# A new table of places for a two-layer kernel whose engines run from orders written out in advance

## The chip, the cores and the metric

The kernel runs on one core of one Trainium2 chip. The metric is the device time of one execution in microseconds (us), from the first to the last instruction with what little lies around it. The data are float32 throughout.

## What is computed

The input x has 128 images of 128 channels and 32 x 32 pixels (1024 pixels to an image). Two layers follow each other.

Layer 0 is attention over the 128 images at each pixel, with four heads, an output projection, a residual and a layer norm. Its result is written to DRAM as `mid`.

Layer 1 works on each image by itself. It multiplies by a 128 x 128 matrix (`cv1`); one branch is a 3 x 3 depthwise convolution with a batch norm and SiLU (`l`); the other is a layer norm over channels followed by a Mamba block over the 1024 pixels. Cut to what matters here, the Mamba block is:

```
xm, z = split(t @ in_proj.T)              # 256 channels each
xm    = silu(conv1d(xm))                  # causal, 4 taps
dt, B, C = split(xm @ x_proj.T)           # 8, 16, 16 columns
dt    = softplus(dt @ dt_proj.T + bias)   # 256 channels
h     = exp(dt * A) * h + dt * B * xm     # over pixels, for 256 channels x 16 states
y     = sum over states of h * C, + xm * D
out   = (y * silu(z)) @ out_proj.T
```

The two branches meet in a last matrix (`cv2`), and x is added.

## The kernel before

Layer 0 (`attention_layer`) is not touched by the change. Layer 1 (`mamba_layer`) goes image by image. The state recurrence of one image has 256 x 16 = 4096 rows of 1024 pixels, cut into 32 **groups** of 128 rows. Group k belongs to a half h of the channels (k < 16: h = 0, else h = 1), to a block nb of four states (k // 4 mod 4) and to a block db of 32 channels (k mod 4). For each group:

- ScalarE makes the decays exp(dt * A) from `dtr`, which holds dt replicated over the states (`decays`, L1058).
- The inputs dt * B * xm come from GpSimd for two groups at once (`inputs(j)` for groups 2j and 2j+1, into `dbu`, L1069), from `dtxr` (dt * xm replicated) and `brep` (B replicated). For nb = 0, that is groups 0 to 3 and 16 to 19, TensorE makes them instead (`inputs_by_tensor`, L1080) from the transposed `dtxT` and the diagonal matrices `bdiag`; then the decays of the group are written into `dbu`.
- VectorE runs the recurrence as a scan (`group`, L1093).
- The product with C (`crep`) is GpSimd's for the groups in `ON_POOL` (`product`, L1100), else VectorE's, right behind the scan (L1095).
- TensorE adds up the products of four groups at a time (`sums`, L1116), and at the end of each half VectorE multiplies by the gate (`gate`, L1125).

`dbu` has two buffers: inputs j overwrite what inputs j-2 (or the decays of groups 2j-4 and 2j-3) left, so inputs j wait for scan 2j-3. `hc`, in which products stand, has eight. PSUM leaves two banks (`banks`, "p_ps" in the profile) for everything else.

The replicated tiles are loaded by DMA from DRAM: dt and dt * xm of one half are stored (`dt_store`, `dtx_store`), and then loaded four times over in sets of four DMAs of 256 KB each: `dtr[0]`, `dtr[1]` (`load_dt`), `dtxr[0]`, `dtxr[1]` (`load_dtx`). B and C are stored with `bc_store` and loaded by `load_b` (brep) and `load_c` (crep). All DMAs are issued by SyncE, in one queue. `x_load` brings the image after the next, `x_again` brings back the present one for its last addition.

All else for the next images goes on beside the recurrence: the outputs of the image before (`o_mm`, `o_copy`, `out_store`), the second part of the next image (`d_mm`, `b_mm`, `a_mm`, `split`, `expm`, `log1p`, `dt_mm`, `dt_copy`, `dtx_mul`, the transposes `t_mm`, `t_copy`, the depthwise `taps`, `z_mm`, `diagonals`), and the first part of the one after it (`cv1_mm`, `squared`, `variance`, `rstd`, `normed`, `xm_mm`, `xm_copy`, `padded`). `dtx_mul` is GpSimd's, `normed` VectorE's, copies and functions are ScalarE's.

No scheduler decides the order; `step` writes it out by hand, once per image, with a loop over k. Each engine runs its instructions in exactly that order. In step k come, one after the other: the operations whose place is below k + 0.3; the scan of group k; the gate; the decays of group k + 2 (with TensorE's inputs); after an odd k GpSimd's inputs for groups k + 3 and k + 4; the operations whose place is below k + 0.6; the product of group k; the loads for which `LOADS_*` names k; the sums for which `SUMS_AT` names k. `PLACES` gives the place of each operation, by its name and its count within the image; an operation whose predecessors aren't in yet, or for which no PSUM bank is free, comes as soon as it may (`Order.put`). The entries of `LOADS_DT` and `LOADS_DTX` are, in order: h = 1 parts 0 and 1 of the present image, h = 0 parts 0 and 1 of the next.

The core of the loop, shortened:

```
for k in range(NG):
    order.put(k + EARLY)
    group(k)
    ...
    if k % 2 and (2 * a < NG or nxt is not None):
        if not by_tensor(2 * a):
            inputs(a % (NG // 2))
    order.put(k + LATE + EARLY)
    product(k)
    for ahead, do, what, at in LOADS:
        if k == at and (nxt is not None or not ahead):
            do(nxt if ahead else im, *what)
```

Of the kernel before, what the change touches and what calls it, by code (L numbers as in the profile page):

```python
# [320 lines left out]
class Bank:  # L321
# [7 lines left out]
EARLY, LATE, LAST = 0.3, 0.3, 0.6  # L329


ON_POOL = [2, 3, 8, 10, 12, 13, 14, 15, 16, 17, 22, 24, 25, 28, 29, 30, 31]
SHARED = 5
SUMS_AT = [6, 9, 11, 19, 20, 23, 29]
GATES_AT = [20, 1]
LOADS_DT = [12, 13, 27, 30]
LOADS_DTX = [15, 18, 31, 31]
LOADS_B = [23, 3, 4]
LOADS_C = [25, 0]
REMADE = 18  # L340

PLACES = {
    "silus": [3.3],
    "o_mm": [5, 10.3],
    "o_copy": [5.01, 10.31],
    "out_store": [5.02, 10.34],
    "d_mm": [5.03],
    "d_copy": [7],
    "t_mm": [7.01, 8, 20.02, 28],
    "t_copy": [7.02, 8.02, 20.03, 28.02],  # L350
    "a_mm": [8.3, 8.01, 28.01, 30],
    "split": [8.31, 8.03, 28.03, 30.01],
    "expm": [8.32, 30.02],
    "b_mm": [9.3],
    "b_copy": [9.31],
    "z_mm": [10.32, 10.35, 16.01, 14],
    "z_copy": [10.33, 11.3, 16.02, 14.01],
    "log1p": [12, 30.03],
    "dt_mm": [12.01, 12.02, 31.61, 31.63],
    "dt_copy": [13.3, 15.3, 31.62, 31.64],  # L360
    "dt_store": [15.31, 31.66],
    "x_load": [16],
    "dtx_mul": [16.3, 31.65],
    "dtx_store": [16.31, 31.67],
    "bc_store": [18],
    "diagonals": [
        26.3, 24.3, 20.32, 18.06, 18.04, 18.07, 22.04, 18.01, 29.3, 18.02, 18.03, 19, 25.3, 24,
        21, 18.05,
    ],
    "taps": [19.01, 19.3, 19.31],  # L370
    "l_copy": [19.32, 19.33],
    "cv1_mm": [20, 22.01, 25.01, 27],
    "squared": [20.01, 22.02],
    "variance": [20.3, 22.31],
    "rstd": [20.31, 23.3],
    "normed": [22, 25],
    "xm_mm": [22.03, 30.04, 25.03, 25.04],
    "xm_copy": [22.3, 31.6, 26, 26.31],
    "padded": [25.02, 27.02],
    "x_again": [27.01],  # L380
}


# [203 lines left out]
def mamba_layer(ctx: ExitStack, tc: tile.TileContext, ident, eps, mid, c, out):  # L587
# [398 lines left out]
    def load_x(b):  # L986
        nc.sync.dma_start(x, mid[ds(b, 1)].rearrange("o c l -> (o c) l"))
# [39 lines left out]
    def on_pool(k):  # L1027
        return k in ON_POOL

# [138 lines left out]

    LOADS = [(i > 1, load_dt, (1 - i // 2, i % 2), v) for i, v in enumerate(LOADS_DT)]
    LOADS += [(i > 1, load_dtx, (1 - i // 2, i % 2), v) for i, v in enumerate(LOADS_DTX)]  # L1170
    LOADS += [(i == 0, load_b, (i,), v) for i, v in enumerate(LOADS_B)]
    LOADS += [(i < 1, load_c, (i,), v) for i, v in enumerate(LOADS_C)]
    SUMS = {v: j for j, v in enumerate(SUMS_AT)}

    def step(b, im, nxt=None, was=None, then=None):
# [23 lines left out]
        if then is not None:  # L1199
            ops.append(Op("x_load", lambda: load_x(then), stored_outputs))  # L1200
            ops += first_part(im, [*reads, ops[-1]], xm_start=SUMS_AT[4] + LAST)

        users = [op for op in ops if op.name == "cv1_mm"] or stored_outputs
        ops.append(Op("x_again", lambda: load_x(b), users))
        order = Order(ops, banks, PLACES)
        for k in range(NG):
# [170 lines left out]
```

## Time and profile before

| | |
|---|---|
| median of 3 runs | 16214.31 us (16213.59 to 16221.85) |
| the profiled execution: time, span | 16207.52 us, 16205.7 us |
| TensorE (PE) busy | 14907.9 us, 92% |
| VectorE (DVE) busy | 14001.0 us, 86% |
| ScalarE (ACT) busy | 11943.2 us, 74% |
| GpSimd (POOL) busy | 13178.7 us, 81%; from slice 8 of 40 on, 90% or more in each |
| DMA | 2187.55 MB, mean 135 GB/s |
| granted TensorE clock | 0.960 |

The profile is of one execution. Layer 0 takes the first seven or so of its 40 slices, and layer 1 the rest, where GpSimd shows 9 tenths in every slice. PE, DVE, ACT, POOL and SP are TensorE, VectorE, ScalarE, GpSimd and SyncE; L1069 is line 1069 of the kernel. In the lines of groups, the numbers after the bar are busy time and the mean of one in ns, then the engine's idle time just before them and what ended it. In the lines of waits: total us, how many times, longest. In a timeline: start, duration, engine, line, operation, tiles, how many in a row, and in brackets the idle time before it and its releaser. "SPq" is SyncE's queue of DMAs, at their issue.

### The profile page before, as it was taken

How to read it: one execution, taken by the hardware profiler on the slowest of the kernel's cores; microseconds unless marked ns; L12 is line 12 of the kernel's file. 1: busy time of each engine (PE TensorE's matmuls, PEld its weight loads, DVE VectorE, ACT ScalarE, POOL GpSimd, SP SyncE). 2: the span in 40 equal slices, each digit the busy share in tenths (PEclk: the TensorE clock that was granted, in tenths of full speed). 3: DMA queues.
4: the chain of work that ended last, by engine and by line, in shares of the span. 5: the costliest groups of instructions: out<-in, count | busy, mean ns of one | idle time of the engine just before them, and what ended most of it. 6: DMA issues, size and time to landing. Idle time of an engine off the chain costs nothing. (4 is left out here: it accounts for less than half of the span.)

```text
span 16205.7 us, 335746 instructions
## 1 busy us (share of the span) xinstructions
PE 14907.9 (92%) x141366; PEld 7196.6 (44%) x141366; DVE 14001.0 (86%) x8882; ACT 11943.2 (74%) x17542; POOL 13178.7 (81%) x4488
## 2 busy tenths in 40 slices
PE   9999999899999999999999999999999999999998
PEld 6666666343444434444444444444444444443443
DVE  7777777698888889999989999989999899889988
ACT  6666666677777777777777777777777777777776
POOL 1222222699999999999999999999999999999999
PEclk9999999899999999999999999999999999999998
DMA  3222221566666666666666666666666666666665
GB/s 57 53 43 53 53 43 33 130 152 153 155 158 155 152 153 156 155 157 157 156 157 157 154 152 154 156 158 157 154 152 154 152 158 155 157 151 152 155 158 131
DMA packets 1175599, 2187.55 MB, mean 135 GB/s; under 512 B 656848, under 2 KB 657888, under 8 KB 1174112
## 3 DMA queue, kind: packets, MB, share of 16 engines
q1 hardware_dynamic: 1174112, 2166.24, 54.5%
q8 instruction: 1114, 18.25, 0.5%
q14 instruction: 373, 3.06, 0.1%
HBM read 1746.30 MB, written 419.43 MB: 134 GB/s over the span
## 5 line engine op out<-in xcount | busy, mean ns | idle before, releaser
L1069 POOL TENSOR_TENSOR dbu<-dtxr,brep 128x2048 f32<-128x2048 f32 x1536 | 6971.2, 4544 | 453.4 <-DMA dtxr<-dtxd 265.7
L1100 POOL TENSOR_TENSOR hc<-hc,crep 128x1024 f32<-128x1024 f32 x2176 | 5122.3, 2374 | 0.0
L1058 ACT ACTIVATE da<-dtr,aneg 128x1024 f32<-128x1024 f32 x2944 | 3283.3, 1117 | 1246.6 <-DVE hc L1093 719.3
L1093 DVE TENSOR_TENSOR_SCAN hc<-da,dbu 128x1024 f32<-128x1024 f32 x1664 | 3753.9, 2278 | 360.5 <-POOL dbu L1069 300.3
L1093 DVE TENSOR_TENSOR_SCAN da<-da,dbu 128x1024 f32<-128x1024 f32 x1280 | 2922.1, 2283 | 357.5 <-POOL dbu L1069 352.6
L1095 DVE TENSOR_TENSOR hc<-da,crep 128x1024 f32<-128x1024 f32 x1792 | 2194.4, 1225 | 161.9 <-PE y_ps L1116 58.9
L1116 PE MATMUL y_ps<-hc,fold 128*32 128x512 f32 x16384 | 2244.8, 646 | 43.3 <-POOL hc L1100 39.2
L1080 PE MATMUL da<-bdiag,dtxT 128*32 128x128 f32 x65536 | 1987.4, 275 | 196.9 <-issue 93.9
L1080 PEld LDWEIGHTS da<-bdiag,dtxT 128*32 128x32 f32 x65536 | 1776.9, 110 | 574.4 <-DVE hc L1093 374.7
L730 PE MATMUL p_ps<-tn,wk 128*128 128x512 f32 x4056 | 1821.2, 596 | 0.0
L1093 DVE TENSOR_TENSOR_SCAN da<-dbu,da 128x1024 f32<-128x1024 f32 x512 | 1172.5, 2290 | 212.4 <-PE da L1080 123.6
L964 ACT ACTIVATE bdiag<-ident,bT 128x128 f32<-128x128 f32 x4096 | 1307.8, 387 | 65.0 <-PE da L1080 64.2
L1093 DVE TENSOR_TENSOR_SCAN hc<-dbu,da 128x1024 f32<-128x1024 f32 x512 | 1145.1, 2275 | 159.4 <-PE da L1080 113.2
L221 POOL COPY xg<-xt 128x512 f32<-128x512 f32 x256 | 269.8, 1055 | 1236.8 <-PE m_ps L217 1205.7
L730 PEld LDWEIGHTS p_ps<-tn,wk 128*128 128x128 f32 x4056 | 752.8, 189 | 1016.6 <-issue 842.3
L1058 ACT ACTIVATE dbu<-dtr,aneg 128x1024 f32<-128x1024 f32 x1024 | 1119.4, 1142 | 112.5 <-DMA dtr<-dtd 105.6
L1116 PEld LDWEIGHTS y_ps<-hc,fold 128*32 128x32 f32 x16384 | 489.3, 115 | 1542.5 <-issue 1186.3
L243 POOL TENSOR_SCALAR yt<-z,nw,nb 128x512 f32<-128x512 f32 x256 | 319.8, 1249 | 1029.6 <-DVE z L242 1029.6
L915 PE MATMUL p_ps<-xpad,dwd 64*64 64x512 f32 x9216 | 1046.0, 592 | 25.6 <-issue 24.8
L790 POOL TENSOR_TENSOR sp<-dt,xm 128x1024 f32<-128x1024 f32 x256 | 613.0, 2395 | 270.8 <-ACT dt L804 264.6
L767 PE MATMUL p_ps<-xp,dtwT 8*128 8x512 f32 x1016 | 643.8, 716 | 204.4 <-ACT dtxT L832 174.4
L203 DVE TENSOR_TENSOR oT<-m_ps,rden 128x512 f32<-128x512 f32 x256 | 177.1, 692 | 575.7 <-ACT rden L202 575.7
(200 smaller groups left out, 22410.7 us busy)
## 6 DMA issues: line engine op xcount, KB each, us to landing
dtr<-dtd SPq DMA_DIRECT2D x2048, 256.0 KB, 5.0
dtxr<-dtxd SPq DMA_DIRECT2D x2048, 256.0 KB, 7.3
crep<-bcd SPq DMA_DIRECT2D x1024, 256.0 KB, 6.7
brep<-bcd SPq DMA_DIRECT2D x1536, 128.0 KB, 5.0
x<-mid SPq DMA_DIRECT2D x256, 512.0 KB, 5.7
dtd<-dt SPq DMA_DIRECT2D x256, 512.0 KB, 4.8
dtxd<-sp SPq DMA_DIRECT2D x256, 512.0 KB, 6.9
xt<-in_x SPq DMA_DIRECT2D x64, 1024.0 KB, 12.0
```

Source lines behind the costliest of these rows:

```text
L730: nc.tensor.matmul(bank.tile, lhsT=wk[:, k, h * P : (h + 1) * P], rhs=tn[:, c * CH + k : (c + 1) * CH + k], start=k == 0, stop=c > 0 and k ...
L767: nc.tensor.matmul(bank.tile, lhsT=dtwT[c * HP + XD : c * HP + NX, h * P : (h + 1) * P], rhs=xp[c * HP + XD : c * HP + NX], start=True, st ...
L790: nc.gpsimd.tensor_mul(sp, dt, im["xm"][h])
L915: nc.tensor.matmul(pair[r] .tile[c * HP : (c + 1) * HP] .rearrange("p (r q) -> p r q", q=HH), lhsT=dwd[rs, k, :], rhs=xpad[rs, y0 : y0 + r ...
L964: nc.scalar.activation(bdiag[:, j, :], ident, AF.Copy, scale=bT[:, j : j + 1])
L1058: nc.scalar.activation(operands(k)[0], dtr[db // 2][:, db % 2, :], AF.Exp, scale=aneg[:, h * NDB + db, nb : nb + 1])
L1069: nc.gpsimd.tensor_mul(dbu[j % 2], dtxr[db // 2], b.unsqueeze(1).to_broadcast([P, 2, L]))
L1080: nc.tensor.matmul(operands(k)[1][n * GD : (n + 1) * GD, tb * P : (tb + 1) * P], lhsT=dtxT[:, tb, db * GD : (db + 1) * GD], rhs=bdiag[:, t ...
L1093: nc.vector.tensor_tensor_scan(dst, a, b, 0.0, ALU.mult, ALU.add)
L1095: nc.vector.tensor_mul(hc[k % 8], dst, crep[nb // 2][:, nb % 2, :])
L1100: nc.gpsimd.tensor_mul(hc[k % 8], hc[k % 8], crep[nb // 2][:, nb % 2, :])
L1116: nc.tensor.matmul(y_ps[db * GD : (db + 1) * GD, chunk(c)], lhsT=fold, rhs=hc[(j * NDB + db) % 8][:, chunk(c)], start=False, stop=nb == NN ...
```

## The change

Only constants change: the groups whose products are GpSimd's, the steps of the sums, the steps of the loads, and the table of places. No instruction is added or taken away; the order on each engine changes. Compared by the built programs, in one image in the middle:

- GpSimd multiplies groups 7, 9 and 26 instead of 8, 10 and 25. Its order by kinds of instruction stays the same but for one: the first dtx_mul comes before product 14 instead of before product 16.
- SyncE's order before: crep[1]; brep[1]; brep[2]; out_store; out_store; dtr[0], dtr[1] (h = 1); dt_store; dtxr[0]; x_load; dtx_store; bc_store; dtxr[1]; brep[0]; crep[0]; x_again; dtr[0], dtr[1]; dtxr[0], dtxr[1] (h = 0 of the next image); dt_store; dtx_store.
- SyncE's order after: brep[2]; brep[1]; crep[1]; bc_store; out_store; out_store; x_load; dtr[0], dtr[1] (h = 1); dt_store; dtxr[0]; dtxr[1]; brep[0]; dtx_store; crep[0]; dtxr[0] (h = 0 of the next image); x_again; dtr[0]; dtr[1]; dtxr[1]; dtx_store; dt_store.
- On TensorE the second o_mm moves from behind sums 1 to behind sums 0, and dt_mm, z_mm, t_mm and a_mm are dealt anew among steps 7 to 16; from step 17 on its order by kinds is the same.
- On ScalarE both first dt_copy come before decay 16 (one stood before decay 16, one behind decay 17), expm and log1p before decay 13 (log1p stood behind it), o_copy of the second chunk before decay 11 (it stood behind decay 12), and the diagonals are spread over steps 18 to 25 instead of 18 to 29.

```diff
-ON_POOL = [2, 3, 8, 10, 12, 13, 14, 15, 16, 17, 22, 24, 25, 28, 29, 30, 31]
+ON_POOL = [2, 3, 7, 9, 12, 13, 14, 15, 16, 17, 22, 24, 26, 28, 29, 30, 31]
 SHARED = 5
-SUMS_AT = [6, 9, 11, 19, 20, 23, 29]
+SUMS_AT = [6, 11, 13, 19, 21, 23, 28]
 GATES_AT = [20, 1]
-LOADS_DT = [12, 13, 27, 30]
-LOADS_DTX = [15, 18, 31, 31]
-LOADS_B = [23, 3, 4]
-LOADS_C = [25, 0]
+LOADS_DT = [13, 13, 27, 29]
+LOADS_DTX = [14, 18, 26, 31]
+LOADS_B = [23, 3, 1]
+LOADS_C = [25, 3]
 REMADE = 18
 
 PLACES = {
+    "o_mm": [2, 8.3],
     "silus": [3.3],
-    "o_mm": [5, 10.3],
-    "o_copy": [5.01, 10.31],
-    "out_store": [5.02, 10.34],
-    "d_mm": [5.03],
-    "d_copy": [7],
-    "t_mm": [7.01, 8, 20.02, 28],
-    "t_copy": [7.02, 8.02, 20.03, 28.02],
-    "a_mm": [8.3, 8.01, 28.01, 30],
-    "split": [8.31, 8.03, 28.03, 30.01],
-    "expm": [8.32, 30.02],
-    "b_mm": [9.3],
-    "b_copy": [9.31],
-    "z_mm": [10.32, 10.35, 16.01, 14],
-    "z_copy": [10.33, 11.3, 16.02, 14.01],
-    "log1p": [12, 30.03],
-    "dt_mm": [12.01, 12.02, 31.61, 31.63],
-    "dt_copy": [13.3, 15.3, 31.62, 31.64],
-    "dt_store": [15.31, 31.66],
-    "x_load": [16],
-    "dtx_mul": [16.3, 31.65],
-    "dtx_store": [16.31, 31.67],
-    "bc_store": [18],
+    "d_mm": [3.31],
+    "d_copy": [5.3],
+    "bc_store": [5.31],
+    "o_copy": [6.3, 8.31],
+    "out_store": [6.31, 8.34],
+    "t_mm": [7, 10, 27.3, 20.03],
+    "t_copy": [7.01, 10.01, 27.32, 20.04],
+    "z_mm": [12, 16, 8.32, 12.3],
+    "z_copy": [12.01, 16.01, 8.33, 12.31],
+    "x_load": [8.35],
+    "b_mm": [9],
+    "b_copy": [9.01],
+    "a_mm": [11, 10.02, 27.31, 30],
+    "split": [11.01, 10.03, 27.33, 30.01],
+    "expm": [11.02, 30.02],
+    "log1p": [11.03, 30.03],
+    "dt_mm": [14.02, 14, 31.62, 31.6],
+    "dt_copy": [14.03, 14.01, 31.63, 31.61],
+    "dtx_mul": [14.04, 31.64],
+    "dt_store": [14.05, 31.66],
     "diagonals": [
...
     ],
-    "taps": [19.01, 19.3, 19.31],
-    "l_copy": [19.32, 19.33],
-    "cv1_mm": [20, 22.01, 25.01, 27],
-    "squared": [20.01, 22.02],
-    "variance": [20.3, 22.31],
-    "rstd": [20.31, 23.3],
-    "normed": [22, 25],
-    "xm_mm": [22.03, 30.04, 25.03, 25.04],
-    "xm_copy": [22.3, 31.6, 26, 26.31],
-    "padded": [25.02, 27.02],
-    "x_again": [27.01],
+    "taps": [19.3, 19.31, 19.32],
+    "l_copy": [19.33, 20],
+    "cv1_mm": [20.01, 22.01, 27.02, 25.04],
+    "squared": [20.02, 22.02],
+    "variance": [20.3, 23.3],
+    "rstd": [20.31, 23.31],
+    "normed": [22, 25.03],
+    "xm_mm": [30.04, 22.03, 27, 26],
+    "xm_copy": [30.05, 23, 27.01, 26.01],
+    "dtx_store": [24, 31.65],
+    "padded": [27.04, 25.05],
+    "x_again": [27.03],
 }
```

More of the change, by code (lines that the diff above doesn't have):

```diff
@@ L366 @@
+    "x_load": [8.35],
[9 more added lines that the diff above has]
+    "dt_store": [14.05, 31.66],
     "diagonals": [
-        26.3, 24.3, 20.32, 18.06, 18.04, 18.07, 22.04, 18.01, 29.3, 18.02, 18.03, 19, 25.3, 24,
-        21, 18.05,
-    ],
@@ L370 @@
-    "taps": [19.01, 19.3, 19.31],
-    "l_copy": [19.32, 19.33],
-    "cv1_mm": [20, 22.01, 25.01, 27],
-    "squared": [20.01, 22.02],
-    "variance": [20.3, 22.31],
-    "rstd": [20.31, 23.3],
-    "normed": [22, 25],
-    "xm_mm": [22.03, 30.04, 25.03, 25.04],
-    "xm_copy": [22.3, 31.6, 26, 26.31],
-    "padded": [25.02, 27.02],
-    "x_again": [27.01],
+        25.01, 18.06, 18.07, 18.01, 18.03, 18, 18.04, 25, 18.02, 21.3, 21.31, 25.02, 20.32, 21,
+        21.01, 18.05,
+    ],
+    "taps": [19.3, 19.31, 19.32],
```

## The prediction

> **What bounds the kernel now.** I read the page's costliest groups first, then the waits, then the timelines of one image. In the groups, GpSimd's two kinds of product stand at the top:
>
> ```profile
> L1069 POOL TENSOR_TENSOR dbu<-dtxr,brep 128x2048 f32<-128x2048 f32 x1536 | 6971.2, 4544 | 453.4 <-DMA dtxr<-dtxd 265.7
> L1100 POOL TENSOR_TENSOR hc<-hc,crep 128x1024 f32<-128x1024 f32 x2176 | 5122.3, 2374 | 0.0
> ```
>
> Per image that is 12 x 4.54 + 17 x 2.37 + two dtx_mul of 2.40 = 99.7 us; they overlap a little in the pipeline and occupy 98.7 us. From one image to the next it is 103.2 us (the 256 gates of L1125 start between 3038.9 and 16194.8 us, two per image: 13155.9 / 127.5). So GpSimd, idle some 4.5 us per image, is the bound, and its idle time is all that a new order can give back. The list of waits says who ends it:
>
> ```profile
> POOL dbu L1069 <- DMA dtxr<-dtxd: 265.7, 256, 3.2
> POOL sp L790 <- ACT dt L804: 264.6, 125, 58.7
> POOL dbu L1069 <- DVE da L1093: 127.4, 100, 20.8
> ```
>
> The first is 2.08 us per image. I call t0 the end of inputs 15 and t1 the end of inputs 7, the last input products of the two halves of an image. GpSimd's timeline of one image shows where the waits lie:
>
> ```profile
> 9093.33 4.54 POOL L1069 TENSOR_TENSOR dbu<-dtxr,brep 128x2048 f32<-128x2048 f32 x1
> ...
> 9113.89 4.55 POOL L1069 TENSOR_TENSOR dbu<-dtxr,brep 128x2048 f32<-128x2048 f32 x1 [2.05 <-DMA dtxr<-dtxd]
> ...
> 9121.53 9.04 POOL L1069 TENSOR_TENSOR dbu<-dtxr,brep 128x2048 f32<-128x2048 f32 x2 [0.76 <-DMA dtxr<-dtxd]
> ...
> 9146.46 4.53 POOL L1069 TENSOR_TENSOR dbu<-dtxr,brep 128x2048 f32<-128x2048 f32 x1
> ...
> 9161.83 2.41 POOL L790 TENSOR_TENSOR sp<-dt,xm 128x1024 f32<-128x1024 f32 x1 [1.53 <-ACT dt L804]
> 9164.72 4.54 POOL L1069 TENSOR_TENSOR dbu<-dtxr,brep 128x2048 f32<-128x2048 f32 x1 [0.48 <-DMA dtxr<-dtxd]
> ```
>
> Here t1 = 9097.87 and t0 = 9150.99. Inputs 10 and 11 wait 2.05 and 0.76 us for dtxr (over 122 images 1.33 and 0.65), dtx_mul 1 waits 1.53 (always), inputs 2 waits 0.48. Over those images t1 to t0 takes 52.7 us and t0 to the next t1 50.5. Next, SyncE's queue:
>
> ```profile
> 9094.64 5.22 SPq L991 DMA_DIRECT2D dtr<-dtd  x8
> 9104.39 0.34 SPq L979 DMA_DIRECT2D dtd<-dt  x1
> 9104.83 2.71 SPq L991 DMA_DIRECT2D dtxr<-dtxd  x4
> 9107.58 0.42 SPq L987 DMA_DIRECT2D x<-mid  x1
> 9109.53 0.34 SPq L979 DMA_DIRECT2D dtxd<-sp  x1
> ...
> 9111.26 2.73 SPq L991 DMA_DIRECT2D dtxr<-dtxd  x4
> ...
> 9144.59 0.35 SPq L987 DMA_DIRECT2D x<-mid  x1
> 9146.63 6.09 SPq L991 DMA_DIRECT2D dtr<-dtd  x8
> 9152.82 6.71 SPq L991 DMA_DIRECT2D dtxr<-dtxd  x8
> ```
>
> and the windows of 2 us with their last two columns, DMA share and GB/s:
>
> ```profile
> 9141.00:9143.00 2.00, 2.00 (x6) 0.91 (x5) 2.00 (x2) 1.05 (x1) 2.00 (x1) 1.00 0.00 0
> ...
> 9149.00:9151.00 2.00, 2.00 (x6) 0.83 (x5) 0.83 (x1) 1.43 (x3) 2.00 (x2) 1.00 1.03 219
> ```
>
> The transfers come in two bursts, t1-3 to t1+22 and t0-6 to t0+28, in which the DMA engines are full at about 220 GB/s, and are idle between. One set of four loads is 1 MiB, 4.8 us in a full queue. So a load's arrival is set by the bytes issued ahead of it.
>
> **What the Trainium skill says.** [...] "DMA: Bandwidth & Descriptors", section on queues, rings and completion order, says that each DMA engine consumes descriptors in ring order; the trace agrees: after t0 the means of the last landings are x -3.0, dtr[0] 2.4, dtr[1] 7.2, dtxr[0] 12.7, dtxr[1] 17.1, in order of issue. The same page, on the anatomy of one DMA, says that semaphore waits happen on the issuing sequencer: a DMA that waits holds all behind it in SyncE's queue. In the trace, dtxr[0] (9104.83) stands behind the dtd store (9104.39), which waits for ScalarE's dt_copy.
>
> **The change, part by part.** No instruction is added or removed; durations stay.
>
> *Groups.* Products 8, 10, 25 become 7, 9, 26. GpSimd's sequence of kinds stays: one product between inputs 5 and 6, one between 6 and 7, one between 14 and 15. VectorE's multiply moves by one group. Slack: product 25 starts at 9144.15; scan 26 will end at 9136.12 (scan 25's start) + 3.46 (scan with multiply) + 2.2 = 9141.8. Sums 1 now needs product 7, which ends where product 8 does (9086.5), while scan 12, which needs sums 1, starts at 9091.4. Zero, hidden by 2 to 3 us.
>
> *dtx_mul 0* moves ahead of products 14 and 15. It needs dt_copy by t1+4.7; the new places (14, before ScalarE's decay 16) give t1+1.7. Zero.
>
> *Second half.* With dt_copy at t1+1.7, the dtd store and dtxr[0] are issued at once instead of at t1+6.5. But the queue still holds both dtr sets: the last of dtr was issued at 9099.44 and took 6.6 us to land. dtr[0]'s issue follows decay 13, at t1-3.8 in the mean now. In the new order ScalarE has decay 12, split, expm and log1p ahead of it in place of o_copy: group 10's multiply ends 9.15 us after scan 7's end, which is t1-18.2; then 1.05 + 1.2 + 0.94 + 0.95 and decay 13's 1.1 make 14.4, so t1-3.8 again. So dtxr[0] gains only the thin spot in the DMA between (0.3 to 0.5 us). dtxr[1] gains more: x_load, the dtxd store and bc_store, 1.1 MiB, leave the place before it, so that it lands 4.8 us after dtxr[0] instead of 7.7, and inputs 11's 0.65 us goes. Inputs 12 gains 0.1 to 0.2 more, until it meets scan 21. Sum about 1.1 us. What is late next: VectorE's second normed, which already waits for ScalarE,
>
> ```profile
> 9135.45 0.75 DVE L708 SCALAR_TENSOR_TENSOR tn<-p_ps,b1c,tn 128x512 f32<-128x512 f32 x1 [0.26 <-ACT tn L702]
> ```
>
> at the end of TensorE's chain taps, sums 3, cv1, variance. That doesn't move; scan 25 follows it, and inputs 14 must wait for scan 25. Now inputs 14 starts 1.05 us after scan 25's end (mean). So the half gains at most 1.05, and **0.9** allowing for scatter.
>
> *First half.* dtxr[0] of the next image moves from step 31 to 26: behind inputs 14, at t0-6.8, into an idle DMA. It can't be late for inputs 2 any more (0.5 us gone). But it and x now stand ahead of dtr[0], which decay 0 needs. Estimate: data flows from t0-5.9 (0.9 after issue, as for the burst at t1), dtxr[0] 4.8, x 1.5 to 2.3, dtr[0] 4.8, landing 0.9 after its data: t0+6.1 to 6.9, against 2.4 now. Scan 0 waits for that decay already:
>
> ```profile
> 9155.85 2.30 DVE L1093 TENSOR_TENSOR_SCAN da<-dbu,da 128x1024 f32<-128x1024 f32 x1 [0.36 <-ACT dbu L1058]
> ```
>
> It moves from t0+4.9 to t0+7.4 (decay 1.1). From scan 0 to scan 7's end: two scans with multiply at 3.47, gate 1.15, two scans at 2.2, three with multiply at 3.46, one scan 2.3: 25.2 us, so t0+32.6. Inputs 5 reuses scan 7's half of dbu; it starts at t0+31.9 here, 32.3 in the mean, with 0.8 us of slack that is now used up. It starts at 32.65, and 18.15 us later is t1: 50.8 instead of 50.5, a loss of **0.35**; at the late end of my estimate 1.1.
>
> *Behind dtx_mul 1*: its 1.53 us hang on scan 31, inputs of group 33, dt_mm, dt_copy, in the same order: stays. brep[2] and brep[1] go ahead of crep[1]; 0.5 MiB instead of 1 stands before brep[1], and it lands earlier; crep[1] at about t0+28.3, first used by VectorE at t0+33.8. bc_store, x_load, dtx_store 0 go to idle stretches. Diagonals come earlier on ScalarE; squared 1 may be 1 us later, its reader has 3. Zero each.
>
> **Sum.** 0.9 - 0.4 = 0.5 us per image, 127 times: 60 us off the profiled execution's 16207.5. The median of the runs, 16214.3, is 6.8 higher, so about **16155**.
>
> **Rivals.** (1) *dtr[0] decides the other way.* If it lands at t0+7.4, scan 7 ends at 33.9, the half costs 1.65 more, and the gain of the other is 0.6 at the low end: 1.05 x 127 = 133 us slower, 16347. The point where it turns is a landing at t0+6.6, half a us from my estimate; for it speaks that nothing hides scan 0, against it that x drains faster than the loads (256 GB/s at a DMA share of 0.76). (2) *Even*: what inputs 11 saves comes back at inputs 5; 16214. That is also what comes of it if dtxr lands no sooner, since dtr is ahead of it before and after. (3) *A larger gain*: dtr[0] by t0+5.3 costs nothing, the 0.5 at inputs 2 stays won: 1.3 x 127 = 165 us, 16050. All of GpSimd's DMA waits, 2.5 x 127 = 318 us, can't be had because of normed.
>
> **Numbers.** A measurement can tell about 0.2%, 32 us, from no change. My case and (3) together 0.48, even 0.18, slower 0.34. Range 16030 to 16325: from somewhat beyond (3) nearly to (1). The faster cases alone: 16035 to 16180.
>
> **What would show it.** Inputs 11 without a DMA wait; inputs 10 still with one of 0.5 to 1 us; inputs 2 without; dtr[0] landing at t0+6 to 7 and VectorE idle 2.5 to 3 us before scan 0 for ScalarE; inputs 5 waiting for VectorE. Wrong if GpSimd waits for brep or crep, if ScalarE's decays 20 to 27 stop VectorE, or if t1 to t0 stays at 52.7.

## The result, and the profile after

The changed kernel takes **16575.5 us** (median, 16569.9 to 16589.1) against 16218.1 us before on the same chip: 1.0222 times as long, 95% interval 1.0209 to 1.0234. The forecast was 60 us faster; it is 357 us slower. The profiled execution took 16589.1 us, its span is 16587.3 us against 16205.7. The granted TensorE clock was 0.963 in it, against 0.960 before, so the clock is not the cause.

I use the forecast's two marks again: t0 is the end of GpSimd's inputs 15, t1 that of inputs 7. Over the 122 images in the middle of the run, means in us:

| | t0 to t1 | t1 to t0 | one image |
|---|---|---|---|
| before | 50.49 | 52.72 | 103.22 |
| after | 51.64 | 54.59 | 106.23 |

So 3.01 us per image are lost: 1.15 in the first half (t0 to t1) and 1.87 in the second (t1 to t0). Times 127 that is 382 us, the difference of the spans. The costliest groups of the changed kernel (busy time, mean ns of one, then the idle time before them and what ended most of it):

```profile
L1069 POOL TENSOR_TENSOR dbu<-dtxr,brep 128x2048 f32<-128x2048 f32 x1536 | 6982.5, 4546 | 818.7 <-DVE da L1093 429.0
L1100 POOL TENSOR_TENSOR hc<-hc,crep 128x1024 f32<-128x1024 f32 x2176 | 5121.1, 2373 | 0.0
```

GpSimd does the same work in the same time, 4546 and 2373 ns an instruction. What has grown is its idle time before the inputs, 818.7 us instead of 453.4, and most of it now ends with VectorE's scan, not with a DMA. The waits of the changed kernel (total, times, longest; lines left out are marked by dots) say the same:

```profile
...
PEld p_ps L915 <- issue: 760.1, 2214, 5.2
...
ACT dbu L1058 <- DMA dtr<-dtd: 522.7, 278, 5.3
...
DVE da L1093 <- ACT dbu L1058: 443.0, 127, 6.4
...
POOL dbu L1069 <- DVE da L1093: 429.0, 167, 20.8
...
DVE hc L1095 <- PE y_ps L1116: 342.0, 126, 8.5
...
PE da L1080 <- issue: 233.0, 142, 3.0
...
POOL dbu L1069 <- DMA dtxr<-dtxd: 225.9, 205, 2.2
...
POOL dbu L1069 <- DVE hc L1093: 152.8, 130, 1.3
```

The same waits in the kernel before, as far as the forecast does not show them:

```profile
...
PE da L1080 <- issue: 93.9, 60, 3.8
...
DVE da L1093 <- ACT dbu L1058: 88.1, 126, 1.9
...
DVE hc L1095 <- PE y_ps L1116: 58.9, 33, 4.4
...
POOL dbu L1069 <- DVE hc L1093: 3.7, 3, 1.5
```

GpSimd's DMA wait fell from 265.7 to 225.9 us, its wait for VectorE's scans rose from 127.4 to 429.0, and the 152.8 is as good as new (3.7 before). Behind VectorE stand ScalarE (443.0; 88.1 before) and TensorE (342.0; 58.9 before). And TensorE stops by itself: "issue" means that the profile shows nothing it waited for, 233.0 us in 142 stops at L1080 (93.9 in 60 before).

One image of the changed kernel, t0 = 9241.81, t1 = 9292.79, the next t0 = 9346.34. VectorE's and GpSimd's timelines (start, duration, in brackets the idle time before it and what ended it):

```profile
9249.37 2.29 DVE L1093 TENSOR_TENSOR_SCAN da<-dbu,da 128x1024 f32<-128x1024 f32 x1 [3.06 <-ACT dbu L1058]
...
9316.67 1.22 DVE L1095 TENSOR_TENSOR hc<-da,crep 128x1024 f32<-128x1024 f32 x1 [1.51 <-PE y_ps L1116]
...
9331.49 0.75 DVE L708 SCALAR_TENSOR_TENSOR tn<-p_ps,b1c,tn 128x512 f32<-128x512 f32 x1 [0.51 <-ACT tn L702]
```

```profile
9274.65 4.52 POOL L1069 TENSOR_TENSOR dbu<-dtxr,brep 128x2048 f32<-128x2048 f32 x1 [1.20 <-DVE hc L1093]
...
9308.27 4.55 POOL L1069 TENSOR_TENSOR dbu<-dtxr,brep 128x2048 f32<-128x2048 f32 x1 [1.53 <-DMA dtxr<-dtxd]
...
9315.08 4.55 POOL L1069 TENSOR_TENSOR dbu<-dtxr,brep 128x2048 f32<-128x2048 f32 x1
...
9321.37 4.55 POOL L1069 TENSOR_TENSOR dbu<-dtxr,brep 128x2048 f32<-128x2048 f32 x1 [1.74 <-DVE da L1093]
```

The first half's loss is the first line of each: scan 0 waits 3.06 us for its decay, and inputs 5 then wait 1.20 for scan 7. In the second half inputs 10 still wait for DMA (1.53), inputs 11 (9315.08) don't wait any more, as forecast, and inputs 12 (9321.37) wait 1.74 us for scan 21, which they did not in the image shown of before. Scan 21 is late because VectorE's multiply of group 20 waited for TensorE (9316.67). So look at TensorE:

```profile
9300.29 2.38 PE L1080 MATMUL da<-bdiag,dtxT 128*32 128x128 f32 x78
9305.22 1.69 PE L1080 MATMUL da<-bdiag,dtxT 128*32 128x128 f32 x50 [2.54 <-issue]
9306.84 7.96 PE L915 MATMUL p_ps<-xpad,dwd 64*64 64x512 f32 x72
9314.73 1.92 PE L1116 MATMUL y_ps<-hc,fold 128*32 128x512 f32 x16
```

In the inputs of groups 18 and 19, after 78 of their 128 matmuls, TensorE stands still for 2.54 us with nothing to wait for. The taps (L915) and sums 3 (L1116) follow, and the multiply of group 20 writes a buffer of `hc` that sums 3 must have read. I call the sum of such stops per image in the inputs of groups 18 and 19 ("inputs 18, 19" in the expectations below) and the taps **TensorE's gaps**. Counted are the steps of over 0.6 us from the start of one matmul to the start of the next: 0.65 us before, 3.64 after. The taps start at t1+13.5 instead of 11.8 and end at t1+23.0 instead of 20.2.

What does TensorE wait for? The DMA view of the window 9302.3 to 9302.6, with packets, MB and share:

```profile
## 3 DMA queue, kind: packets, MB, share of 16 engines
q1 hardware_dynamic: 17, 0.06, 103.8%
q8 instruction: 1, 0.02, 28.9%
```

Among the data (q1) a DMA of kind "instruction" starts there. In the whole run there are 1114, with 18.25 MB, 16 KB each. They fit TensorE: it executes 141,366 matmuls and as many weight loads, and the Trainium skill ("Trainium Architecture — The Big Picture", The software stack) gives 64 bytes for an instruction, from which I estimate 282,732 x 64 bytes = 18.1 MB. (The same section speaks of the streams as brought in when the program is loaded; here this one comes in blocks of 256 instructions during the run.) This fetch runs from 9302.48 to 9303.86 in the trace, and TensorE goes on at 9305.22, 1.36 us after its end. That is no accident: of the stops in these operations that are longer than 1 us, all 153 in the changed kernel and all 40 in the kernel before end 1.15 to 1.75 us after such a fetch ended, with only two or three such fetches in the 20 us from t1 on. And when all of TensorE's instructions in the trace are numbered from the first, the one with which it goes on is in all 193 stops the third or fourth of a block of 256: each stop stands at the edge of a block as large as one fetch. TensorE had run out of instructions.

SyncE's queue suggests why the fetches are late. The data for t1 to t1+20 are in it sooner:

```profile
9289.13 5.40 SPq L991 DMA_DIRECT2D dtr<-dtd  x8
9294.96 0.34 SPq L979 DMA_DIRECT2D dtd<-dt  x1
9295.39 6.80 SPq L991 DMA_DIRECT2D dtxr<-dtxd  x8
```

Both sets of dtxr are issued right behind dtr, from t1+3.0 to t1+9.8 in the mean; before, they came from t1+6.5 to t1+15.7. The profile counts the fetches among the packets of the same 16 DMA engines. This is **theory A**: the data now stand in the queue while TensorE runs through its shortest instructions (the inputs of groups 16 to 19: 256 matmuls and as many weight loads in 8 us of work, two blocks), and the fetches come late. **Theory B**: the new orders of the engines make the second half longer by themselves. The experiments had to tell these apart, and settle the first half.

### The profile page after: what moved, and what is told of

It reads as the page before. It is cut to its first block, busy times and chain, and to the rows that moved or that the text cites. A ratio compares the mean times of both kernels' runs of the same rounds, so it can differ in the third digit from the quotient of the medians.

```text
span 16587.3 us, 335744 instructions
## 1 busy us (share of the span) xinstructions
PE 14866.6 (90%) x141366; PEld 7183.3 (43%) x141366; DVE 13979.7 (84%) x8882; ACT 11928.1 (72%) x17542; POOL 13180.3 (79%) x4488
## 3 DMA queue, kind: packets, MB, share of 16 engines
q8 instruction: 1114, 18.25, 0.5%
q14 instruction: 374, 3.06, 0.1%
## 5 line engine op out<-in xcount | busy, mean ns | idle before, releaser
L1069 POOL TENSOR_TENSOR dbu<-dtxr,brep 128x2048 f32<-128x2048 f32 x1536 | 6982.5, 4546 | 818.7 <-DVE da L1093 429.0
L1100 POOL TENSOR_TENSOR hc<-hc,crep 128x1024 f32<-128x1024 f32 x2176 | 5121.1, 2373 | 0.0
L1058 ACT ACTIVATE da<-dtr,aneg 128x1024 f32<-128x1024 f32 x2944 | 3283.6, 1116 | 1293.9 <-DVE hc L1093 753.6
L1095 DVE TENSOR_TENSOR hc<-da,crep 128x1024 f32<-128x1024 f32 x1792 | 2194.5, 1225 | 443.8 <-PE y_ps L1116 342.0
L1080 PE MATMUL da<-bdiag,dtxT 128*32 128x128 f32 x65536 | 2037.7, 276 | 522.6 <-issue 233.0
L1116 PE MATMUL y_ps<-hc,fold 128*32 128x512 f32 x16384 | 2174.1, 639 | 37.9 <-POOL hc L1100 35.3
L1080 PEld LDWEIGHTS da<-bdiag,dtxT 128*32 128x32 f32 x65536 | 1791.5, 111 | 929.5 <-DVE hc L1093 362.3
L1093 DVE TENSOR_TENSOR_SCAN da<-dbu,da 128x1024 f32<-128x1024 f32 x512 | 1173.2, 2291 | 702.3 <-ACT dbu L1058 443.0
L1058 ACT ACTIVATE dbu<-dtr,aneg 128x1024 f32<-128x1024 f32 x1024 | 1120.9, 1142 | 665.5 <-DMA dtr<-dtd 522.7
L964 ACT ACTIVATE bdiag<-ident,bT 128x128 f32<-128x128 f32 x4096 | 1251.4, 387 | 190.0 <-PE da L1080 188.9
L915 PE MATMUL p_ps<-xpad,dwd 64*64 64x512 f32 x9216 | 1113.5, 612 | 104.3 <-issue 103.2
L1093 DVE TENSOR_TENSOR_SCAN hc<-dbu,da 128x1024 f32<-128x1024 f32 x512 | 1142.6, 2272 | 42.3 <-PE da L1080 22.4
L1116 PEld LDWEIGHTS y_ps<-hc,fold 128*32 128x32 f32 x16384 | 450.0, 113 | 1570.3 <-issue 1265.5
L870 PE MATMUL p_ps<-xm,xpT 128*64 128x512 f32 x1016 | 392.5, 901 | 435.1 <-ACT xm L842 435.1
L915 PEld LDWEIGHTS p_ps<-xpad,dwd 64*64 64x64 f32 x9216 | 370.4, 137 | 762.0 <-issue 760.1
```

Of the source, the lines that this page charges most:

```text
L870: nc.tensor.matmul(bank.tile[c * HP : (c + 1) * HP], lhsT=xpT[:, h, :], rhs=im["xm"][h][:, chunk(c)], start=h == 0, stop=h == DI2 - 1,)
L915: nc.tensor.matmul(pair[r] .tile[c * HP : (c + 1) * HP] .rearrange("p (r q) -> p r q", q=HH), lhsT=dwd[rs, k, :], rhs=xpad[rs, y0 : y0 + r ...
L964: nc.scalar.activation(bdiag[:, j, :], ident, AF.Copy, scale=bT[:, j : j + 1])
L1058: nc.scalar.activation(operands(k)[0], dtr[db // 2][:, db % 2, :], AF.Exp, scale=aneg[:, h * NDB + db, nb : nb + 1])
L1069: nc.gpsimd.tensor_mul(dbu[j % 2], dtxr[db // 2], b.unsqueeze(1).to_broadcast([P, 2, L]))
L1080: nc.tensor.matmul(operands(k)[1][n * GD : (n + 1) * GD, tb * P : (tb + 1) * P], lhsT=dtxT[:, tb, db * GD : (db + 1) * GD], rhs=bdiag[:, t ...
```

## The experiments

All times and ratios are against the kernel before on the same chip; the means are over the same 122 images. "Gaps" are TensorE's, and the last two columns are counted from t1.

| kernel | time, us | ratio, 95% interval | t0 to t1 | t1 to t0 | gaps | taps end | inputs 12 |
|---|---|---|---|---|---|---|---|
| before | 16218 | 1 | 50.49 | 52.72 | 0.65 | 20.2 | 27.7 |
| after | 16576 | 1.0222 (1.0209 to 1.0234) | 51.64 | 54.59 | 3.64 | 23.0 | 29.6 |
| after, dtxr[0] back | 16486 | 1.0162 (1.0145 to 1.0179) | 50.74 | 54.63 | 3.19 | 23.0 | 29.6 |
| after, dtxd store back | 16510 | 1.0179 (1.0162 to 1.0196) | 51.58 | 53.98 | 2.96 | 22.4 | 29.0 |
| after, four DMAs back | 16415 | 1.0115 (1.0098 to 1.0132) | 50.76 | 54.10 | 2.55 | 22.5 | 29.1 |
| after, dt back too | 16328 | 1.0070 (1.0053 to 1.0086) | 50.56 | 53.61 | 0.79 | 21.6 | 28.6 |
| after, paced | 16572 | 1.0220 (1.0203 to 1.0237) | 50.79 | 55.32 | 0.66 | 20.6 | 29.8 |
| after, fewer bytes | 16124 | 0.9946 (0.9929 to 0.9962) | 51.58 | 50.93 | 0.09 | 19.3 | 25.9 |
| before, fewer bytes | 16033 | 0.9884 (0.9868 to 0.9900) | 50.93 | 50.92 | 0.03 | 19.4 | 25.9 |
| before, dtxr[0] at 26 | 16437 | 1.0133 (1.0116 to 1.0150) | 51.69 | 53.14 | 0.82 | 20.6 | 28.2 |
| before, groups | 16456 | 1.0147 (1.0130 to 1.0164) | 50.49 | 54.74 | 0.42 | 22.1 | 29.8 |
| before, x and B, C ahead | 16427 | 1.0130 (1.0113 to 1.0146) | 50.78 | 54.23 | 0.51 | 22.0 | 29.2 |
| before, x early | 16542 | 1.0197 (1.0180 to 1.0214) | 52.85 | 53.22 | 0.70 | 21.2 | 28.2 |
| before, x_again behind | 16345 | 1.0077 (1.0061 to 1.0094) | 52.17 | 52.16 | 0.49 | 19.7 | 27.2 |

**The first half: dtxr[0] of the next image.** Taken back alone in the changed kernel, and moved alone in the kernel before:

```
after:   LOADS_DTX = [14, 18, 26, 31]  ->  [14, 18, 31, 31]
before:  LOADS_DTX = [15, 18, 31, 31]  ->  [15, 18, 26, 31]
```

> The changed kernel with one entry put back: dtxr[0] of the next image is loaded at step 31 again, behind both dtr sets, not at step 26. Theory (the queue ahead of dtr[0]): dtr[0] lands at t0+2.4 again, scan 0 starts at t0+5 and not at t0+8.2, and t0 to t1 goes from 51.6 back to about 50.5 us: 1.1 x 127 = 140 us less than the changed kernel, 16435. Rival (the new order on ScalarE and VectorE makes the first half late by itself, xm_copy ahead of decay 0): the first half stays at 51.6, 16575.

> The kernel before with one entry changed: dtxr[0] of the next image is loaded at step 26. Theory (the queue ahead of dtr[0]): dtr[0] lands at t0+6.4, first half 51.6 instead of 50.5, about 140 us slower than before, 16358. Rival (it isn't the queue): inputs 2 no longer wait 0.5 us for dtxr, 60 us faster, 16158.

Taken back, t0 to t1 falls from 51.64 to 50.74; done alone, it rises from 50.49 to 51.69. The fourth and last load of dtr[0] lands at t0+6.87 and 6.86 with the move, and at 3.60 and 3.04 without (means of the 91 or 92 images in which the trace has its landing). VectorE's wait for decay 0 (most of the line shown), in the changed kernel with dtxr[0] back and in the kernel before with it moved:

```profile
DVE da L1093 <- ACT dbu L1058: 132.9, 152, 1.8
```

```profile
DVE da L1093 <- ACT dbu L1058: 445.1, 149, 6.1
```

Both runs show the same cause: this one load makes 0.9 of the first half's 1.15 us in the changed kernel, and more than the whole in the one before. What makes the other 0.25 us is open. In the kernel before the move also costs 0.4 us in the second half, for which I have no separate run.

**The second half: the order of SyncE's DMAs.** First only the dtxd store of dtx_mul 0, which SyncE must wait for, ahead of dtxr[1] again; then with it x_load, bc_store and dtxr[0] of the next image; then also dt_mm, dt_copy, dtx_mul and the dtd store, so that dtxr[0] is issued at t1+7.1:

```
"dtx_store": [24, 31.65]             ->  [16.31, 31.65]      (all three)
LOADS_DTX = [14, 18, 26, 31]         ->  [14, 18, 31, 31]    (second; third: 15 for 14)
"x_load": [8.35], "bc_store": [5.31] ->  [16.3], [18]        (second; third: [16], [18])
"dt_mm": [14.02, 14, ...]            ->  [12.01, 12.02, ...] (third)
"dt_copy": [14.03, 14.01, ...]       ->  [13.3, 15.3, ...]   (third)
"dtx_mul": [14.04, ...], "dt_store": [14.05, ...] -> [16.3, ...], [15.31, ...]  (third)
```

> The changed kernel with dtx_store 0 put back to place 16.31, ahead of dtxr[1], so that SyncE waits for GpSimd's dtx_mul before it issues dtxr[1]. Theory (TensorE's instruction fetches stand in the DMA engines behind the data, and eight dtxr loads issued in a row at t1+3 to t1+8 make that queue deep just where TensorE needs 640 instructions in 20 us): TensorE's gaps in the inputs of groups 18 and 19 and in taps go from 2.9 us per image to under 1.5, taps end 1 us earlier or more, t1 to t0 goes from 54.6 to about 53.2: 180 us less than the changed kernel, 16395. Rival (the new order of dt_mm, z_mm and products makes taps late whatever the DMAs do): taps end at t1+23 as in the changed kernel and inputs 11 waits 0.5 us for dtxr again: 16575 to 16640.

> The changed kernel with the order of its DMAs put back in both bursts: dtxr[0] of the next image at step 31, dtx_store 0 at 16.31, x_load at 16.3, bc_store at 18; groups, sums and all other places stay new. Theory (both losses come from the order of the DMAs): first half 50.5, second 52.7 to 53, so 16220 to 16260. Rival (the new order of the engines costs by itself): 16450 or more.

> The changed kernel with the order of SyncE's DMAs of before between the loads of crep[0] and brep: dtxr[0] of the second half again behind dt_copy at step 15, x_load, the dtxd store and bc_store ahead of dtxr[1], dtxr[0] of the next image at step 31; dt_mm, dt_copy and dtx_mul go back to their old steps with it. The groups, the sums and the rest of the new table stay. Theory A (TensorE is stopped because its instructions are fetched through DMA engines that are full of data, and the new order of DMAs puts the data where the fetches for inputs 18, 19 and the taps fall): with the data back, TensorE's gaps there fall from 3.6 us per image to under 1, the taps start at t1+12 instead of 13.5, t1 to t0 takes 52.7 to 53.0, and the time is 16230 to 16270. Theory B (the new orders of the engines, without the DMAs, make the second half longer): gaps of 2.5 or more, taps at t1+13.5, t1 to t0 at 54, 16400.

The gaps fall step by step, 3.64, 2.96, 2.55, 0.79, as more data are issued later. The first two fell short of what A expected of them (gaps under 1.5 us; 16220 to 16260), and the last step takes most: with it the dtd store and dtxr[0] are issued at t1+6.7 and 7.1, in place of 3.7 and 4.1. That is what A says. But the third kernel should have come to 16230 to 16270 and stays at 16328: z_mm stands ahead of the inputs of group 16 on TensorE in this mixture and waits for ScalarE, so that they start at t1+4.4 instead of 2.5, and scan 16 starts at t1+6.4 instead of 4.8. So the gaps speak for A, the time doesn't decide.

**The queue alone.** One place moved, so that SyncE waits for dtx_mul 0 before it issues the dtd store and both sets of dtxr, with the first half's load back too. The orders of TensorE, VectorE, ScalarE and GpSimd are the changed kernel's:

```
"dtx_store": [24, 31.65]      ->  [14.045, 31.65]
LOADS_DTX = [14, 18, 26, 31]  ->  [14, 18, 31, 31]
```

> The changed kernel with two places altered: the dtxd store of dtx_mul 0 stands ahead of the dtd store (so that SyncE waits for dtx_mul 0, which ends near t1+7, before it issues dtxr[0] and dtxr[1] of the second half, in place of t1+3 and t1+6), and dtxr[0] of the next image is back at step 31. Groups, sums, x_load, bc_store and all orders of TensorE, VectorE, ScalarE and GpSimd stay as changed. Theory A (what counts is how far ahead of the engines the data are queued while TensorE runs inputs 18, 19 and the taps): TensorE's gaps fall from 3.6 us per image (3.2 with dtxr[0] alone back) to under 1.2, the taps start at t1+12, t1 to t0 takes 52 to 52.8, t0 to t1 50.7, and the time is 16160 to 16260. Theory B (the new orders of the engines): gaps of 2.5 or more and taps at t1+13.5 as with the dtxd store behind dtxr[0], t1 to t0 at 54, 16410 to 16490.

The gaps fall to 0.66 and the taps start at t1+12.4 and end at 20.6: as A has it, and against B. But the time, which A put at 16160 to 16260, doesn't fall. dtxr[0], now issued at t1+8.5, comes late for inputs 10, which start at t1+18.1 instead of 15.3. GpSimd's waits in this kernel:

```profile
POOL dbu L1069 <- DMA dtxr<-dtxd: 524.3, 199, 5.2
...
POOL dbu L1069 <- DVE da L1093: 162.5, 206, 20.8
```

The wait has gone back from VectorE (429.0 after) to the DMA (225.9 after). Data early stop TensorE, data late stop GpSimd.

**Fewer bytes.** The direct test: every instruction of the four engines in its place, but less data in the queue; the rows that are not loaded keep the data of earlier images. It was made in both tables:

```
 def by_channel(dst, src, sets=GN):
-    for n in range(GN):
+    for n in range(sets):
...
 # load_dt, part 1, and load_dtx, both parts: of h = 1, from the fifth image on
+    sets = 1
```

> The changed kernel, with every instruction in its place on TensorE, VectorE, ScalarE and GpSimd, but from the fifth image on dtr[1], dtxr[0] and dtxr[1] of the second half are loaded by one of their four DMAs only (the other rows keep old data): 2.25 MiB less in the queue between t1 and t1+20. Theory A: with less data in the DMA engines the fetches come in time, TensorE's gaps in inputs 18, 19 and the taps fall from 3.6 us per image to under 1, the taps start at t1+12, inputs 12 at t1+27.5 or earlier, t1 to t0 takes 52 to 52.7 (the wait of 1.3 us at inputs 10 is gone too), and the time is 16290 to 16350. Theory B: the gaps stay over 3 and the taps at t1+13.5; t1 to t0 above 54, and 16500 to 16575.

> The kernel before with the same cut as in the changed kernel with fewer bytes: from the fifth image on dtr[1], dtxr[0] and dtxr[1] of the second half are loaded by one of their four DMAs only (the other rows keep old data). It compares the two tables with the data out of TensorE's way; the changed one took 50.93 us from t1 to t0 there. Theory A (the second half's loss is the data in the queue and nothing else): t1 to t0 is the same here, 50.6 to 51.2, TensorE's gaps under 0.2 us, t0 to t1 stays at 50.5, and the time is 15950 to 16020. Theory B (the new orders of the engines cost something in this half besides): t1 to t0 at 50.3 or less, 15920 or less. Theory C (they gain something that the gaps hide): t1 to t0 at 51.4 or more, 16040 or more.

With the data out of the way the gaps are gone (0.09 and 0.03), and the second half, shorter than A expected of the changed kernel (52 to 52.7), is 50.93 us with the new table and 50.92 with the old. The whole chain agrees: the taps start at t1+11.33 and 11.36, scan 21 at 23.48 and 23.49, inputs 12 at 25.93 in both. The waits of the changed kernel with fewer bytes (lines from L1058 on are one further here, so L1081 is L1080, and L1096 the multiply):

```profile
POOL dbu L1070 <- DVE da L1094: 126.6, 158, 20.8
...
POOL dbu L1070 <- DMA dtxr<-dtxd: 67.2, 78, 1.9
...
DVE hc L1096 <- PE y_ps L1117: 44.9, 67, 8.1
...
PE da L1081 <- issue: 22.8, 26, 2.6
```

TensorE's 233.0 us of stops have become 22.8, the multiply's wait for sums 3 44.9 instead of 342.0, GpSimd's wait for VectorE's scans is back at 126.6 instead of 429.0. The fetches themselves show the delay. For the blocks of 256 instructions that TensorE enters between t1+5 and t1+20, I took the time from its entry into the block before to the start of the block's own fetch: the median is 2.42 us before, 4.35 after, 2.30 in the paced kernel, and 1.00 and 0.50 with fewer bytes. The inputs of two groups are such a block, and take about 3.9 us (1.95 for 64 matmuls, in the same image).

So A holds: without these data the new orders of the engines cost nothing in this half and bring nothing; the 1.87 us come only with the data in the queue. (This run takes away GpSimd's DMA waits together with TensorE's stops. That it is the stops which make the loss is shown by the chain above, from the taps to inputs 12, and by the DMA waits, which had not grown: 225.9 us after, 265.7 before.) The old table came out at 16033, a little above what A gave, since its first half grew by 0.44 us; why, no run here shows.

**Parts by themselves in the kernel before.** The groups alone, and three other places for x and for B and C, in the hope of the gain that the forecast saw in the second half:

```
groups:              ON_POOL, SUMS_AT as changed
x and B, C ahead:    "x_load": [16] -> [10.35];  "bc_store": [18] -> [9.4]
x early:             o_mm [2, 8.3], o_copy [5.01, 8.31], out_store [5.02, 8.34],
                     x_load [8.35], bc_store [9.4]
x_again behind:      "x_again": [27.01] -> [31.655]
```

> The kernel before with the changed kernel's groups alone (products 7, 9 and 26 on GpSimd in place of 8, 10 and 25, and the steps of the sums that go with them). The prediction costs this at nothing: both halves within 0.15 us, 16200 to 16235. If the groups are part of the loss (the last product of a set of four and the sums come later): 16300 or more.

> The kernel before, with x_load and bc_store ahead of the loads of dtr (steps 10.35 and 9.4), so that dtxr[1] of the second half has 0.6 MiB less in front of it; the dtxd store, which waits for dtx_mul, stays ahead of it. The prediction's reading: inputs 11's wait of 0.65 us goes, t1 to t0 falls to 52.1, 16140. Theory A: dtxr[1] is issued 1.5 us earlier into a queue that is still full; if TensorE's gaps grow by more than 0.65 us from the present 0.65, the gain is eaten up: t1 to t0 at 52.7 to 53.3, 16220 to 16300.

> The kernel before with the changed kernel's early x_load and bc_store only: o_mm at steps 2 and 8.3, x_load at 8.35, bc_store at 9.4, so that the x load lands before the loads of dtr begin, and 1 MiB less stands ahead of dtxr[1] of the second half, while the dtxd store, which waits for dtx_mul near t1+11.7, still does. The prediction's step for the second half, without its early dtxr: inputs 11's wait of 0.65 us goes, TensorE's gaps stay at 0.65 or below, t1 to t0 at 52.0 to 52.2, and the time is 16130 to 16160. If the space that x leaves only moves the data closer to the fetches: gaps over 1.2, t1 to t0 at 52.7 or more, 16213 to 16300.

> The kernel before, with x_again issued behind the four sets of loads for the next image instead of ahead of them. All four sets then start with 0.5 MiB less in front. If arrival is set by the bytes ahead alone: dtr[0] lands 1.5 us earlier, the wait of inputs 2 (0.5 us per image) goes and nothing else moves: t0 to t1 50.0, 16155. If earlier data meet TensorE's fetches elsewhere, the first half stays at 50.5 or grows: 16219 or more.

All four are slower, each by a wait of its own; with x and B, C ahead and with x early the time lies above every range that was expected. With the groups alone VectorE's scan waits 3 us per image for sums 1, which now stand at step 11 of TensorE's old order:

```profile
DVE hc L1093 <- PE y_ps L1116: 381.3, 126, 3.8
```

(18.6 us in the changed kernel, whose places give them room.) With x and B, C ahead, the x load waits for out_store and is issued at t1-3.6, right in front of dtr[0], whose first load then lands at t1+1.9 instead of -0.6; scan 16 is 2 us late. With x early, a scan waits 4.8 us per image for a decay: ScalarE comes to o_copy first and waits there for the second o_mm. And with x_again behind the loads, dtr[0] lands only 0.2 us earlier (fourth load at t0+2.84; 3.04 before), and decay 0 starts as before (t0+3.90; 3.94), so x had hardly been a hindrance, while o_mm now waits for x and GpSimd for brep:

```profile
PEld p_ps L1136 <- DMA x<-mid: 400.6, 111, 4.7
...
POOL dbu L1069 <- DMA brep<-bcd: 203.5, 103, 3.3
```

In that last kernel the second half is 0.56 us shorter than before (52.16), but the first is 1.68 longer. None of the kernels that load all their data beats the one before.

## Why the prediction was wrong, point by point

- **What bounds the kernel** was right: GpSimd's time an instruction is unchanged, and all that changed is its idle time before the inputs.
- **First half.** The chain was right: dtr[0] lands behind dtxr[0] and x, scan 0 waits for decay 0, from scan 0's start to scan 7's end it takes 25.16 us (25.2 forecast), inputs 5 wait for VectorE, and 18.16 us more lead to t1 (18.15). **The term that was mis-sized** is dtr[0]'s landing. The forecast allowed t0+6.1 to 6.9; scan 0 at t0+7.4 and a turning point at 6.6, "half a us from my estimate", take its early end. The fourth load landed at t0+6.87, decay 0 started 0.13 us later and took 1.15, and scan 0 started at 8.18. So the way from landing to scan, 1.3 us, was right, and the loss is 1.15 us instead of 0.35, as the forecast said for "the late end of my estimate" (1.1). Its landings of the kernel before were read too early, too: the trace lacks two of dtr[0]'s four landings in half of the images, and the 2.4 is the mean of the last one that is there. The fourth load alone gives 3.04.
- **Second half, dtxr.** Inputs 11 without a wait: right; they start at t1+22.15 instead of 22.84. Inputs 10 still with a DMA wait: right; but dtxr[0], which was to gain 0.3 to 0.5 us, gained nothing (fourth load at t1+15.17; 15.11 before). 4 MiB lie behind each other in the queue, and their order decides what lands when.
- **The step that failed** is "That doesn't move", said of TensorE's chain taps, sums 3, cv1, variance, normed. I took TensorE's order by kinds from step 17 on as the same, and so its time as the same. The taps end 2.84 us later, since TensorE runs out of instructions (3.64 us of gaps per image, 0.65 before), and inputs 12 start 1.85 us later, which is all of the half's 1.87. That "the dtd store and dtxr[0] are issued at once instead of at t1+6.5" was costed as a gain only; what a deeper queue does to other users of the DMA engines was not asked. The profile before did have the sign: 60 stops of TensorE at L1080 released by "issue", 93.9 us, and a queue of kind "instruction".
- **A second step left out**: which reader of `hc` stands between. I asked of inputs 12 only that scan 21 be done in time, and didn't follow scan 21 back: it stands behind group 20's multiply, which waits for sums 3, behind the taps (342.0 us after).
- **What was costed at nothing**: groups, diagonals, brep and crep cost nothing in the changed kernel's second half (it is equal in both tables once the data are away), and GpSimd's wait for brep is 0.8 us in the whole run. In the first half they may have a part in the 0.25 us that dtxr[0] does not explain. The groups are not free by themselves: in the old table they cost 240 us, since sums 1 come too late there. The zero needs the new places around them.
- **Rivals.** The slower one, dtr[0], had the right place and seven tenths of its price (1.15 of 1.65 us), but it is less than two fifths of the loss. The larger part was not among the rivals at all. The text did say what would prove it wrong, t1 to t0 staying at 52.7; it rose to 54.6.

## What to carry to other kernels

A load that is issued earlier isn't free because it waits in a queue: ask who else uses the DMA engines, TensorE's instruction fetches among them, and look for stops released by "issue" in a stretch of many short matmuls. "Same order" on an engine is not "same time": follow the last wait back to its source, through buffers that are reused, before a chain is said not to move. And in an order written out by hand one entry tried alone measures the entry with its neighbours: leave the order and take the data away to see what the data cost.

## What the runs showed of the hardware

- TensorE's instructions come in 16 KB blocks by DMA during the run, 1114 of them. Those that start between t1 and t1+20 of the changed kernel take 0.9 to 1.5 us (median 1.3). When one is late, TensorE stands still at the edge of a block, and goes on 1.15 to 1.75 us after the fetch has ended (193 stops in two kernels). The sum of such stops is 0.65 us per image in the kernel before, 3.64 after, and at most 0.09 with 2.25 MiB less data between t1 and t1+20. The fetch starts later with more data in the queue (medians of 0.50 to 4.35 us, above); what holds it up inside a DMA engine no run here shows.
- These stops and the DMA waits together cost the second half of the kernel before 52.72 - 50.92 = 1.8 us per image. No order of the same data tried here got more than 0.56 of that back, and that one lost more in the first half.
- A decay that waits for the last of four loads starts 0.13 us after its landing, in the mean of 92 images of the changed kernel.
